# Forming a spectral unit's matrices on ScalarE and GpSimd during the first stage of a two-layer kernel, instead of on VectorE between the layers

## The chip, the cores and the metric

The kernel runs on one core of a Trainium2 chip. The metric is the device time of one execution in microseconds (us); the median of seven executions is compared. Engines are called by the profile's short names: PE (TensorE), ACT (ScalarE), DVE (VectorE), POOL (GpSimd), and SP, the engine whose queue issues the DMAs.

## The reference, cut to what matters

Two layers work on a tensor of 4 images, 128 channels and 64x64 pixels. Layer 0 is a convolutional front with a learned order of patches and a selective scan; layer 1 is a second scan with 256 states and then a spectral unit. The spectral unit has four branches (the first 1/1, 1/2, 1/4 and 1/8 of the sequence), each with matrices of its own, and the branches are added with four weights:

```python
s = sigma ** 0.25
out = einsum('btkd,k,kde->bte', U_plus, s, M_plus[i]) + einsum('btkd,k,kde->bte', U_minus, s, M_minus[i])
y_soft = softmax(log_weights + gumbel)
weights = one_hot(argmax(y_soft), 4) - y_soft + y_soft
out = sum over branches i of weights[i] * padded(out_i)
```

A token in the first eighth of the sequence belongs to all four branches, one in the last half to one only. So what the kernel needs for each filter k is, for each of four segments of the sequence, the weighted sum of the matrices of the branches that reach it, once for plus and once for minus, times sigma[k] to the power 0.25. It stores their sum and their difference. These matrices depend on the weights alone, not on x.

## The kernel before, in words

`conv_attn_hybrid` runs four parts in a row.

- `layer0_front` loops over the 4 images. For each it loads x (`xs`, L108), takes statistics on DVE (L111 to L125) and one power on POOL (`rs`, L127), writes the normalised image `xg` (DVE, L129), transposes it on PE and takes more statistics from PSUM (L149 to L157), takes another power on POOL (`r1`, L161), and then does two convolutions on PE (L96), each of eight tiles of 128x512. ACT empties each tile of PSUM through Gelu (L176 for the first convolution, L196 for the second). PSUM has four buffers for these tiles, so the matmuls of tile i need the buffer that ACT emptied of tile i-4. The second convolution needs the mean over all eight Gelu tiles (L181). Scores, an order and a gather by matmul (L206 to L258) end the image. The order of instructions on each engine is set here by a scheduler, which fills from the program in the order of its readiness; once built it is fixed, and each engine works through its own list in order.
- `layer0_scan` has an order written out by hand (`manual_schedule`). It ends with a store of `x2` (L430).
- `spectral_weights` forms the matrices. It loads three small vectors (L616 to L619) and, by some twenty DVE instructions of up to 128x4, gets the four branch weights `wt`; POOL takes the power of sigma (`sig`, L645). `branch_sums` (L647) forms running sums over the four branches with one multiplication and three multiply-adds on DVE. It is called once for the three matrices of `M_u` (to `mue`, stored as `mud`), and for each of 16 filters twice (plus and minus, tile `raw` to tile `sums`). Then DVE multiplies `sums` by `sig` (L668), adds and subtracts the two halves (L670, L671, tile `pq`), and SP stores both to DRAM as `pqd` (L673). `raw`, `sums` and `pq` have two buffers each.
- `layer1` again has an order written out by hand: eight weight and data loads, a projection, and then 8192 steps. Each step runs a scan of 128x1024 on DVE (L1097); POOL forms the scan's input for two steps at a time (L1085), and ACT its factors (L1094). The spectral unit's matmuls (L1045, L989) run beside the scan at a pace that the program sets, and read `pqd` (L956) and `mud` (L903) from DRAM.

Of the kernel before, what the change touches and what calls it, by code (L numbers as in the profile page):

```python
# [8 lines left out]
F32 = mybir.dt.float32  # L9
AF = mybir.ActivationFunctionType  # L10
ALU = mybir.AluOpType
# [6 lines left out]


@with_exitstack  # L20
def layer0_front(ctx: ExitStack, tc, ident, half, w, x, xnt, perm_t):

# [1 line left out]
    nc = tc.nc  # L26
    cp = ctx.enter_context(tc.tile_pool(name="a_c", bufs=1))
# [73 lines left out]
    def by_patch(t, oy):  # L101

        return t.rearrange("c (py px oy ox) -> c oy py px ox", px=16, oy=4, ox=4)[:, oy]

    for b in range(NB):

        xs = xp.tile([128, L], F32, tag="xs", name="xs")
        nc.sync.dma_start(xs, x[b])  # L108
        st = sm.tile([128, 8, 6], F32, tag="st", name="st")
        for q in range(8):  # L110
            nc.vector.bn_stats(st[:, q, :], xs[:, bass.ts(q, 512)])  # L111
# [61 lines left out]
        sums = sm.tile([128, 8], F32, tag="sums", name="sums")  # L173
# [426 lines left out]
NK = 16  # L600


@with_exitstack
def spectral_weights(ctx: ExitStack, tc, sigma, m_u, m_plus, m_minus, log_w, gumbel, pqd, mud):

    nc = tc.nc
    cp = ctx.enter_context(tc.tile_pool(name="w_c", bufs=1))  # L610
    mp = ctx.enter_context(tc.tile_pool(name="w_m", bufs=2))


    lw = cp.tile([128, 4], F32, name="lw")
    gb = cp.tile([128, 4], F32, name="gb")
    nc.sync.dma_start(lw, log_w.partition_broadcast(128))  # L616
    nc.sync.dma_start(gb, gumbel.partition_broadcast(128))
    sig = cp.tile([128, NK], F32, name="sig")
    nc.sync.dma_start(sig, sigma.partition_broadcast(128))  # L619
    nc.vector.tensor_tensor(lw, lw, gb, ALU.add)  # L620
    top = cp.tile([128, 1], F32, name="top")
    nc.vector.tensor_reduce(top, lw, AX, ALU.max)
    nc.vector.tensor_scalar(lw, lw, top, None, ALU.subtract)
    soft = cp.tile([128, 4], F32, name="soft")
    tot = cp.tile([128, 1], F32, name="tot")
    nc.scalar.activation(soft, lw, AF.Exp, accum_out=tot)
    nc.vector.reciprocal(tot, tot)
    nc.vector.tensor_scalar(soft, soft, tot, None, ALU.mult)
    nc.vector.tensor_reduce(top, soft, AX, ALU.max)
    hard = cp.tile([128, 4], F32, name="hard")  # L630
    nc.vector.tensor_scalar(hard, soft, top, None, ALU.is_equal)
    seen = cp.tile([128, 1], F32, name="seen")
    free = cp.tile([128, 1], F32, name="free")
    nc.vector.tensor_copy(seen, hard[:, 0:1])
    for i in range(1, 4):

        nc.vector.tensor_scalar(free, seen, -1.0, 1.0, ALU.mult, ALU.add)
        nc.vector.tensor_tensor(hard[:, i : i + 1], hard[:, i : i + 1], free, ALU.mult)
        nc.vector.tensor_tensor(seen, seen, hard[:, i : i + 1], ALU.max)
    wt = cp.tile([128, 4], F32, name="wt")  # L640
    nc.vector.tensor_tensor(wt, hard, soft, ALU.subtract)
    nc.vector.tensor_tensor(wt, wt, soft, ALU.add)
    quarter = cp.tile([128, NK], F32, name="quarter")
    nc.vector.memset(quarter, 0.25)
    nc.gpsimd.tensor_tensor(sig, sig, quarter, ALU.pow)  # L645

    def branch_sums(dst, src):  # L647

        nc.vector.tensor_scalar(dst[:, 3], src[:, 0], wt[:, 0:1], None, ALU.mult)
        for i in range(1, 4):  # L650
            nc.vector.scalar_tensor_tensor(
                dst[:, 3 - i], src[:, i], wt[:, i : i + 1], dst[:, 4 - i], ALU.mult, ALU.add
            )

    mu = mp.tile([128, 4, 3, 128], F32, name="mu", bufs=1)
    for i in range(4):
        nc.sync.dma_start(mu[:, i], m_u[i].rearrange("k d e -> d k e"))
    mue = mp.tile([128, 4, 3, 128], F32, name="mue", bufs=1)
    branch_sums(mue, mu)
    nc.sync.dma_start(mud, mue)  # L660
    for k in range(NK):
        raw = mp.tile([128, 2, 4, 128], F32, tag="raw", name="raw")
        nc.sync.dma_start(raw[:, 0], m_plus[:, k].rearrange("i d e -> d i e"))
        nc.sync.dma_start(raw[:, 1], m_minus[:, k].rearrange("i d e -> d i e"))
        sums = mp.tile([128, 2, 4, 128], F32, tag="sums", name="sums")
        for side in range(2):
            branch_sums(sums[:, side], raw[:, side])
        nc.vector.tensor_scalar(sums, sums, sig[:, k : k + 1], None, ALU.mult)  # L668
        pq = mp.tile([128, 2, 4, 128], F32, tag="pq", name="pq")
        nc.vector.tensor_tensor(pq[:, 0], sums[:, 0], sums[:, 1], ALU.add)  # L670
        nc.vector.tensor_tensor(pq[:, 1], sums[:, 0], sums[:, 1], ALU.subtract)  # L671
        for side in range(2):
            nc.sync.dma_start(pqd[k, side], pq[:, side])  # L673


@with_exitstack
# [564 lines left out]
@with_exitstack  # L1241
def conv_attn_hybrid(ctx: ExitStack, tc, w, out):
    nc = tc.nc
    const = ctx.enter_context(tc.tile_pool(name="const", bufs=1))
    dram = ctx.enter_context(tc.tile_pool(name="dram", bufs=1, space=DRAM))
    ident = const.tile([128, 128], F32, name="ident")
    make_identity(nc, ident)
    half = const.tile([128, 32], F32, name="half")
    nc.vector.memset(half, -0.5)
    x2 = dram.tile([NB, 128, L], F32, name="x2")  # L1250
    x3 = dram.tile([NB, 128, L], F32, name="x3")
    x = w["x"]
    with tc.tile_pool(name="ordered", bufs=1) as pool:
        xnt = dram.tile([NB, 128, 3 + L], F32, name="xnt")
        perm_t = pool.tile([128, NB, 2, 256], F32, name="perm_t")
        layer0_front(tc, ident, half, w, x, xnt, perm_t)
        layer0_scan(tc, ident, w, x, xnt, perm_t, x2)
    pqd = dram.tile([NK, 2, 128, 4, 128], F32, name="pqd")
    mud = dram.tile([128, 4, 3, 128], F32, name="mud")
    spectral_weights(  # L1260
        tc, w["sigma"], w["M_u"], w["M_phi_plus"], w["M_phi_minus"], w["log_weights"], w["gumbel"], pqd, mud
    )
    layer1(
        tc, ident, half, w["W_in"], w["W_delta"], w["W_B"], w["W_C"], w["W_out"], w["A"], w["phi"], pqd, mud,
        x2, x3, out,
    )
# [48 lines left out]
```

## Time and profile before

| what | value |
|---|---|
| median of 7 runs | 22131.32 us (22126.83 to 22139.19) |
| the profiled execution's own time | 22126.83 us |
| its span in the profile | 22125.0 us |
| busy: PE, DVE, ACT, POOL | 80%, 92%, 71%, 91% |
| `layer0_front` in the profile | 0 to about 776 us |
| `layer0_scan` | about 776 to 3002 us |
| `spectral_weights` | about 3001 to 3083 us |
| `layer1` | about 3083 us to the end |

The profiled execution is the fastest of the seven, 4.49 us under the median; its span is 1.8 us shorter than its time. A line such as "L471 POOL TENSOR_TENSOR v<-dx,bcb 128x1024 f32<-128x1024 f32 x512 | 1207.9, 2359 | ..." gives the line of the program, the engine, the operation, output and input with shape, the number of instructions, their busy time in us, the mean of one in ns, and after the second bar how long the engine sat idle before them and for whom. In the timeline, a line gives the start in us, the length in us, the engine and the instruction, and in brackets the idle time ahead of it and what ended it.

### The profile page before, as it was taken

The page shows a single profiled execution, that of the slowest core. Times are in us where ns is not written, and L with a number is a line of the kernel's source. Part 1 is how long each engine was busy: PE and PEld are TensorE (multiplying, and loading weights), DVE is VectorE, ACT ScalarE, POOL GpSimd, SP SyncE. Part 2 cuts the span into 40 slices and gives each one's busy share as a digit, 9 for nine tenths or more (in the row PEclk, how much of TensorE's full clock was granted, in tenths as well). Part 3 has the DMA queues.
Part 4 walks back from the last instruction along what each step waited for, and adds up shares of the span by engine and source line. Part 5 has one row for each costly group of instructions (what it writes and reads, how often), then busy time and mean ns, then how long its engine had stood idle before and what let it go on. Part 6 is the DMA issues. An engine that isn't in the chain of part 4 may idle for free.

```text
span 22125.0 us, 292872 instructions
## 1 busy us (share of the span) xinstructions
PE 17753.2 (80%) x99156; PEld 7770.0 (35%) x99156; DVE 20448.6 (92%) x11842; ACT 15727.5 (71%) x28971; POOL 20186.5 (91%) x5932
## 2 busy tenths in 40 slices
PE   8788844474867888886858888869598899999999
PEld 4444421131323333342323333324233334434344
DVE  3588879999999999999999999999999999999993
ACT  0477747777777777777777777777777777777773
POOL 0477759999999999999999999999999999999993
PEclk9899976586988999997979999979699999999999
DMA  0255544464656777675657777757577677777775
GB/s 27 78 139 140 140 136 151 151 197 151 206 186 200 218 222 218 218 220 180 213 173 217 220 219 218 220 179 229 164 226 222 218 233 233 232 230 230 229 226 153
DMA packets 2399971, 4238.15 MB, mean 192 GB/s; under 512 B 778200, under 2 KB 1235968, under 8 KB 2395136
## 3 DMA queue, kind: packets, MB, share of 16 engines
q1 hardware_dynamic: 2398464, 4219.40, 62.3%
q8 instruction: 781, 12.80, 0.2%
q14 instruction: 726, 5.95, 0.1%
HBM read 3600.52 MB, written 617.88 MB: 191 GB/s over the span
## 4 chain that ended last, share of the span: by engine, by line
DVE 50%; POOL 17%; PE 13%; ACT 10%; issue 7%; DMA 3%; SPq 0%; DVEq 0%; POOLq 0%; ACTq 0%
DVE s L1097 43%; POOL v L1085 16%; ACT da L1094 6%; PE conv L1045 5%; DVE states L493 3%; PE conv L96 2%; DMA yd<-ye 2%; PE yp L1114 2%; DVE p L497 2%; PE fin L989 1%; ACT f L485 1%; PE y L509 1%; PE mm L402 0%; ACT ye L1120 0%; ACT t L764 0%
## 5 line engine op out<-in xcount | busy, mean ns | idle before, releaser
L1085 POOL TENSOR_TENSOR v<-u,dlb 128x2044 f32<-128x2044 f32 x4096 | 18346.0, 4526 | 105.1 <-DMA dlb<-delta 81.0
L1097 DVE TENSOR_TENSOR_SCAN s<-da,v 128x1024 f32<-128x1024 f32 x8192 | 18055.4, 2268 | 380.3 <-ACT da L1094 308.2
L1094 ACT ACTIVATE da<-dlb,at 128x511 f32<-128x511 f32 x16384 | 11299.5, 690 | 2062.5 <-DVE s L1097 1597.2
L1045 PE MATMUL conv<-strip,tok 128*128 128x512 f32 (+3 forms) x20480 | 8640.2, 551 | 4.0 <-DMA strip<-in_phi 3.9
L1114 PE MATMUL yp<-s,c 128*32 128x256 f32 x65536 | 5015.8, 437 | 2971.5 <-DVE s L1097 1623.8
L1045 PEld LDWEIGHTS conv<-strip,tok 128*128 128x128 f32 x20480 | 3685.1, 192 | 4131.9 <-issue 3749.5
L1114 PEld LDWEIGHTS yp<-s,c 128*32 128x32 f32 x65536 | 1983.8, 121 | 6760.0 <-issue 1838.0
L1089 ACT COPY v<-vf 128x4 f32<-128x4 f32 x4096 | 813.5, 199 | 2259.3 <-DVE s L1097 2134.2
L471 POOL TENSOR_TENSOR v<-dx,bcb 128x1024 f32<-128x1024 f32 x512 | 1207.9, 2359 | 429.5 <-DVE states L493 425.5
L989 PE MATMUL fin<-conved,pq 128*128 128x512 f32 (+1 forms) x3200 | 1422.3, 540 | 11.9 <-ACT conved L1056 3.3
L493 DVE TENSOR_TENSOR_SCAN states<-f,v 128x1024 f32<-128x1024 f32 x512 | 1176.1, 2297 | 173.1 <-ACT f L485 124.0
L1120 ACT COPY ye<-yp 128x512 f32<-128x512 f32 x2048 | 1186.5, 579 | 142.9 <-DMA yd<-ye 125.0
L485 ACT ACTIVATE f<-dt,an 128x255 f32<-128x255 f32 x2048 | 973.4, 476 | 420.3 <-DVE states L493 369.6
L509 PE MATMUL y<-p,ident 128*128 128x512 f32 x2048 | 1003.9, 619 | 149.8 <-DVE p L497 144.6
L1056 ACT COPY conved<-conv 128x512 f32<-128x512 f32 x1344 | 778.5, 579 | 341.8 <-PE conv L1045 340.4
L497 DVE TENSOR_TENSOR p<-states,bcb 128x1024 f32<-128x1024 f32 x512 | 627.0, 1225 | 41.1 <-DVE states L493 2.2
L989 PEld LDWEIGHTS fin<-conved,pq 128*128 128x128 f32 x3200 | 532.1, 194 | 225.3 <-issue 163.5
L509 PEld LDWEIGHTS y<-p,ident 128*128 128x128 f32 x2048 | 367.3, 194 | 679.9 <-issue 358.3
L127 POOL TENSOR_TENSOR rs<-sq,half 128x1 f32<-128x1 f32 x4 | 2.2, 561 | 486.2 <-DVE sq L125 486.2
L402 PE MATMUL mm<-ow,yg 128*32 128x128 f32 x2048 | 282.0, 297 | 106.9 <-ACT om L406 105.4
L402 PEld LDWEIGHTS mm<-ow,yg 128*32 128x32 f32 x2048 | 236.0, 138 | 212.9 <-ACT om L406 128.4
L1005 DVE TENSOR_TENSOR xo<-xo,fin 128x512 f32<-128x512 f32 x32 | 21.3, 666 | 300.8 <-PE fin L997 300.8
(232 smaller groups left out, 6265.2 us busy)
## 6 DMA issues: line engine op xcount, KB each, us to landing
dlb<-delta SPq DMA_DIRECT2D x4096, 512.0 KB, 4.1
strip<-in_phi SPq DMA_DIRECT2D x1536, 448.0 KB, 4.8
yd<-ye SPq DMA_DIRECT2D x2048, 256.0 KB, 4.0
bcb<-bcd SPq DMA_DIRECT2D x1024, 256.0 KB, 4.2
strip<-in_phi SPq DMA_DIRECT2D x1024, 256.0 KB, 4.3
pq<-pqd SPq DMA_DIRECT2D x1088, 64.0 KB, 3.8
yt<-yd SPq DMA_DIRECT2D x4096, 4.0 KB, 3.3
pq<-pqd SPq DMA_DIRECT2D x256, 128.0 KB, 4.0
```

The source lines that it names most:

```text
L471: nc.gpsimd.tensor_tensor(v, ready[n][2][:, :, bass.ts(i, SUB)].unsqueeze(1).broadcast_to((128, 2, 2, SUB)), bc[:, 0].unsqueeze(2).broadca ...
L485: nc.scalar.activation(factors[j % 2][:, a, k, 1:], ready[n][1][:, k, SUB * i + 1 : SUB * i + SUB], AF.Exp, scale=an[:, k, 2 * g + a : 2 * ...
L493: nc.vector.tensor_tensor_scan(states.rearrange(flat), factors[j % 2].rearrange(flat), v.rearrange(flat), 0.0, ALU.mult, ALU.add)
L497: nc.vector.tensor_tensor(p, states, bc[:, 1].unsqueeze(2).broadcast_to((128, 2, 2, SUB)), ALU.mult)
L509: nc.tensor.matmul(t.rearrange("p k t -> p (k t)"), ident, p[:, a].rearrange("p k t -> p (k t)"), start=g == 0 and a == 0, stop=False, ski ...
L989: nc.tensor.matmul(fin[:, bass.ds(c0, w)], pq[:, n, :], u[:, bass.ds(c0, w)], start=begin and n == 0, stop=end and not partly, skip_group_ ...
L1045: nc.tensor.matmul(ps[:, skip:], tok[:, 1 - r if side else r, j, :], strip[:, bass.ds(c0 - lo, TS - skip)], start=src == sources[0] and j ...
L1085: nc.gpsimd.tensor_tensor(v[:, :, :, 1:], ready[0][:, :, 1:].unsqueeze(1).broadcast_to((128, VD, 2, TS - 1)), dl[:, :, 1:].unsqueeze(2).br ...
L1094: nc.scalar.activation(da[:, h, 1:], dl[:, d % VD, 1:], AF.Exp, scale=at[:, h, d : d + 1])
L1097: nc.vector.tensor_tensor_scan(s[:, d % GD].rearrange("p h t -> p (h t)"), da.rearrange("p h t -> p (h t)"), v[:, d % VD].rearrange("p h t ...
L1114: nc.tensor.matmul(yp[i // 2][bass.ts(q, 32), i % 2], c[:, h, t], s[:, :, h, t], start=h == 0, stop=h == 1)
L1120: nc.scalar.copy(ye, yp[j].rearrange("p i d t -> p i t d"))
```

## The change

The matrices are formed inside `layer0_front`. `spectral_weights` becomes a generator that yields after the `M_u` matrices and after each filter; the loop over images asks it for five pieces in each image, right after the load of that image. Its pools now live as long as the front's. The multiplications go from DVE to ACT (`Copy` with a scale, two sides at once, 128x256), with the branch weight and the power of sigma multiplied beforehand into a small tile `both`, so that the multiplication by `sig` alone falls away; the additions go to POOL, in place in `sums`, and so do the final sum and difference. The DRAM tensors are unchanged but are made earlier. The small computation of `wt` is unchanged and stays on DVE, now in the front.

```diff
-def layer0_front(ctx: ExitStack, tc, ident, half, w, x, xnt, perm_t):
+def layer0_front(ctx: ExitStack, tc, ident, half, w, x, xnt, perm_t, pqd, mud):
...
+    matrices = spectral_weights(
+        ctx, tc, w["sigma"], w["M_u"], w["M_phi_plus"], w["M_phi_minus"], w["log_weights"], w["gumbel"], pqd, mud
+    )
     for b in range(NB):
         xs = xp.tile([128, L], F32, tag="xs", name="xs")
         nc.sync.dma_start(xs, x[b])
+        for _ in range(5):
+            next(matrices, None)
...
-@with_exitstack
-def spectral_weights(ctx: ExitStack, tc, sigma, m_u, m_plus, m_minus, log_w, gumbel, pqd, mud):
+def spectral_weights(ctx, tc, sigma, m_u, m_plus, m_minus, log_w, gumbel, pqd, mud):
...
-    def branch_sums(dst, src):
-
-        nc.vector.tensor_scalar(dst[:, 3], src[:, 0], wt[:, 0:1], None, ALU.mult)
+    both = cp.tile([128, 4, NK], F32, name="both")
+    for i in range(4):
+        nc.vector.tensor_scalar(both[:, i, :], sig, wt[:, i : i + 1], None, ALU.mult)
+
+    def branch_sums(dst, src, weight):
+
+        for i in range(4):
+            nc.scalar.activation(dst(3 - i), src(i), AF.Copy, scale=weight(i))
         for i in range(1, 4):
-            nc.vector.scalar_tensor_tensor(
-                dst[:, 3 - i], src[:, i], wt[:, i : i + 1], dst[:, 4 - i], ALU.mult, ALU.add
-            )
+            nc.gpsimd.tensor_tensor(dst(3 - i), dst(3 - i), dst(4 - i), ALU.add)
...
-    branch_sums(mue, mu)
+    branch_sums(lambda r: mue[:, r], lambda i: mu[:, i], lambda i: wt[:, i : i + 1])
     nc.sync.dma_start(mud, mue)
+    yield
     for k in range(NK):
...
-        for side in range(2):
-            branch_sums(sums[:, side], raw[:, side])
-        nc.vector.tensor_scalar(sums, sums, sig[:, k : k + 1], None, ALU.mult)
+        branch_sums(lambda r: sums[:, :, r], lambda i: raw[:, :, i], lambda i: both[:, i, k : k + 1])
         pq = mp.tile([128, 2, 4, 128], F32, tag="pq", name="pq")
-        nc.vector.tensor_tensor(pq[:, 0], sums[:, 0], sums[:, 1], ALU.add)
-        nc.vector.tensor_tensor(pq[:, 1], sums[:, 0], sums[:, 1], ALU.subtract)
+        nc.gpsimd.tensor_tensor(pq[:, 0], sums[:, 0], sums[:, 1], ALU.add)
+        nc.gpsimd.tensor_tensor(pq[:, 1], sums[:, 0], sums[:, 1], ALU.subtract)
         for side in range(2):
             nc.sync.dma_start(pqd[k, side], pq[:, side])
+        yield
...
+        pqd = dram.tile([NK, 2, 128, 4, 128], F32, name="pqd")
+        mud = dram.tile([128, 4, 3, 128], F32, name="mud")
         perm_t = pool.tile([128, NB, 2, 256], F32, name="perm_t")
-        layer0_front(tc, ident, half, w, x, xnt, perm_t)
+        layer0_front(tc, ident, half, w, x, xnt, perm_t, pqd, mud)
         layer0_scan(tc, ident, w, x, xnt, perm_t, x2)
-    pqd = dram.tile([NK, 2, 128, 4, 128], F32, name="pqd")
-    mud = dram.tile([128, 4, 3, 128], F32, name="mud")
-    spectral_weights(
-        tc, w["sigma"], w["M_u"], w["M_phi_plus"], w["M_phi_minus"], w["log_weights"], w["gumbel"], pqd, mud
-    )
```

In the built program, the scheduler does not spread the sixteen filters over the four images as the loop asks for them. All sixteen stand inside the first image on every engine:

- ACT: the four copies for `mue`, 24 copies (filters 0 to 5), the table load and the first Gelu tile of convolution 1; then, between the Gelu tiles, 8 copies (filters 6, 7), tile 1, 8 (8, 9), tile 2, 12 (10 to 12), tile 3, 9 (13, 14 and a quarter of 15), tile 4, 3, and tiles 5 to 7.
- POOL: the power of sigma, `rs` of image 0, the three additions for `mue`, filters 0 to 5 (three additions and the two for `pq` each), `r1` of image 0, filters 6 to 15, and only then `rs` of image 1.
- SP: the load of image 0, the small vectors, `mu`, `raw` of filters 0 and 1, the load of image 1, then stores and loads mixed: the stores of filters 0 and 1 ahead of the loads of filters 2, 3 and 4; the stores of 2 and 3 ahead of the load of 5; those of 4 ahead of 6 and 7; of 5 ahead of 8; of 6 and 7 ahead of 9; and so on to the last stores, all ahead of the first image's own store `xnt`.
- DVE: about twenty small instructions between the statistics of image 0 and its transposes' statistics.
- At the other end, the first weight load of `layer1` stands just ahead of the store of `x2`, and the other loads just after it.

## The prediction

> **What bounds the kernel now.** I read the chain of waits first: it says which engine each stage hangs on. DVE and POOL carry most of it in `layer1`, but the change touches only two short stages, so I asked for busy times by stretch: image 0's first convolution, the gap after it, and the stretch between the layers.
>
> ```profile
> DVE 50%; POOL 17%; PE 13%; ACT 10%; issue 7%; DMA 3%; SPq 0%; DVEq 0%; POOLq 0%; ACTq 0%
> ```
> ```profile
> core 0: us, PE busy (x) PEld busy (x) DVE busy (x) ACT busy (x) POOL busy (x), PEclk, DMA share, GB/s
> 44.00:109.30 65.30, 65.23 (x144) 28.06 (x144) 22.23 (x102) 6.99 (x17) 5.45 (x1) 0.96 0.00 0
> 109.30:112.40 3.10, 0.60 (x4) 0.43 (x4) 1.69 (x8) 3.05 (x5) 0.00 (x0) 1.00 0.00 0
> ...
> 3001.60:3083.30 81.70, 0.00 (x0) 0.00 (x0) 68.74 (x200) 0.30 (x2) 2.91 (x1) 0.52 0.73 238
> ```
>
> Between the layers PE does nothing for 81.7 us, ACT and POOL next to nothing: DVE alone works, 68.7 us of it. In the convolution PE is full, and ACT and POOL have 58 and 60 us to spare. The waits of the stretch between the layers and its timeline tell what holds `layer1` back:
>
> ```profile
> DVE sums L649 <- DMA raw<-in_M_phi_plus: 6.1, 13, 0.6
> ...
> DVE ones L717 <- DMA pqd<-pq: 2.3, 1, 2.3
> ```
> ```profile
> 3001.79 0.37 SPq L430 DMA_DIRECT2D x<-xs  x1
> ```
> ```profile
> 3080.28 0.68 DVE L671 TENSOR_TENSOR pq<-sums 128x512 f32<-128x512 f32 x1
> 3083.28 0.17 DVE L717 MEMSET ones<- 128x128 f32 x1 [2.32 <-DMA pqd<-pq]
> ...
> 3083.42 0.33 SPq L707 DMA_DIRECT2D win<-in_W_in  x1
> ...
> 3086.32 0.47 SPq L783 DMA_DIRECT2D t<-x  x1
> ```
>
> `layer1` starts when the last `pqd` store lands, and its first piece of work is the load of `t` at 3086.32. Everything before it is in series.
>
> **What the skill says.** (1) GPSIMD Engine Reference, Elementwise: side-by-side cycle accounting: an f32 add of 2048 per partition takes 4497 ns. The trace agrees, 4526 ns for 128x2044 (L1085). (2) PSUM, Engine vs sequencer instructions: the queues of ScalarE, VectorE and GpSimd are strictly first in, first out. So a Gelu tile behind matrix copies waits for whatever those wait for. The trace shows no instruction of these engines overtaking. (3) GPSIMD Engine Reference, Specifications: GpSimd shares its SBUF interfaces with VectorE. No run here shows a slowdown from it: L378 takes 2348 ns and L471, beside DVE's scan, 2359. (4) TensorE, What's actually happening: after some microseconds of idleness PE runs at half its clock until it has been busy again. The trace agrees: after the thin stretch of 20.7 us ahead of image 1's convolution, its first weight loads are 0.85 us apart, then 0.43; after the 3.1 us ahead of convolution 2 there is none of it.
>
> **The change, part by part.**
>
> *What is removed.* `layer1`'s seven first loads need no `pqd` now. In the built order they follow the `x2` store of 3001.79, one of them ahead of it. Five at 0.51 us (the spacing at 3083.8 to 3086.3) lie between store and `t`: 3001.8 + 0.4 + 5 x 0.51 = 3004.7, so 81.6 us sooner. The 1 MB store in front of them on the DMA engines takes at most 2.3 us at the 440 GB/s of the start's loads; I take half: **80.5 us gained** (79.3 to 81.6). If `layer1`'s memory were released only with that store's landing (3.84 us in the chain), 78 are left.
>
> *Small DVE work in the front.* The twenty instructions for `wt` and `both` cost 0.15 to 0.23 us each. Of those ahead of `xg`, six fall into DVE's waits for PE and POOL (0.7 us each); seven do not: 1.4 us. Five more among the copies to `xp`, 1.0, and four for `both`, 0.8. Image 0's convolution starts 3.2 us late. POOL's power of sigma (2.9 us) runs while DVE still takes statistics, before `rs` is due. `wt` is ready at 31.2 + 1.4 + 1.0, about 34; `both` at 36.
>
> *The price of one filter.* POOL, from these rows:
>
> ```profile
> L471 POOL TENSOR_TENSOR v<-dx,bcb 128x1024 f32<-128x1024 f32 x512 | 1207.9, 2359 | 429.5 <-DVE states L493 425.5 <-DMA bcb<-bcd 3.5
> ...
> L161 POOL TENSOR_TENSOR r<-ve,half 128x32 f32<-128x32 f32 x4 | 21.8, 5444 | 108.7 <-DVE ve L160 108.7
> ```
>
> 2359 ns for 1024 and 4526 for 2044 give 2.12 ns an element and 0.18 us fixed; dependent additions in the timeline stand 0.08 us further apart. So an addition of 256 takes 0.80 us, one of 512 1.27: 3 x 0.80 + 2 x 1.27 = 4.94 us. ACT: 4 copies at 0.48 (128x255 in L485 takes 476 ns) = 1.9 us. SP: 0.92 for two loads, 0.94 for two stores, `raw` landing 3.1 us after its issue, all as before. POOL is the slow stage: ACT may be two filters ahead (two `sums` buffers), no more.
>
> *Walking the built order.* `mue`: two copies of 0.56, three additions of 1.07: POOL is through at 38.5. Filters 0 and 1 end at 48.4. The loads for filter 2 stand behind their stores on SP: issued by 49.6, landed 52.7, copied, so POOL idles 5.3 us; filters 2 to 5 end at 74.0 (with 0.4 us more of idling). `r1`, 5.45 us, ends at 79.4; its followers on DVE (8.3 us of normalising, 3.7 of statistics) are done by 92, 20 us before they are needed. Filters 6 to 13 take 40.4 us (0.1 each of idling from the same SP order): 119.8.
>
> ACT's Gelu tiles wait in that line. In the profile before, they are:
>
> ```profile
> 54.77 0.69 ACT L176 ACTIVATE f<-conv,b 128x512 f32<-128x512 f32 x1 [0.52 <-PE conv L96]
> ...
> 109.28 0.70 ACT L176 ACTIVATE f<-conv,b 128x512 f32<-128x512 f32 x1 [7.01 <-PE conv L96]
> ```
>
> Tile 0 is now emptied at 73 (behind filter 5), tile 1 at 78, tile 2 at 96, tile 3 at 107. PE needs their buffers for tiles 4 to 7 at 81, 89, 97 and 104.5: PE stalls once, by some 3 us, ahead of tile 7. The end is set by ACT: filter 15's first copy needs the `sums` of filter 13 (119.8) and follows filter 14's copies, 121.2; tile 4 at 121.9, three copies, tiles 5 to 7: the last Gelu ends at **125.7 instead of 110.0, 15.7 us late**. The 3.2 us of the late start are inside this. Convolution 2 needs the mean over all eight tiles, so this is on the path. PE idles some 12 us there instead of 3.1; half clock then costs what it costs convolution 1 (65.2 us against 8 x 7.79 = 62.3): **2.9**. Sum: 18.6.
>
> *What is free.* POOL ends filter 15 at 130, 80 us before `rs` of image 1 (213.6); SP's last store is out by then too, 80 us before `xnt`. Images 1 to 3, `layer0_scan` and `layer1`'s loop keep their instructions and order: nothing.
>
> *Sum.* 80.5 - 18.6 = **61.9 us less** than the profiled execution: 22126.8 becomes 22064.9. That execution is 4.5 us under the median, so the median becomes 22069.4.
>
> *Unseen prices, from both sides.* No row shows POOL additions of 256 with two strides, or beside DVE's two-port copies and statistics. Below: at 0.8 of my prices the last Gelu ends at 114.2, and under 0.75 it ends at 113 whatever they are, as the late convolution sets it. Above: at 1.1, 131.5; at 1.25, 141.7. A gain below zero in DVE's or SP's waits is excluded: nothing there gets less. `layer1`'s DRAM addresses shift; its loop is 19,040 us long, and the runs shown spread by 6 us either side, which I allow it.
>
> **The rivals.**
>
> *A. As walked: 22069* (POOL prices at 0.85 to 1.25 of mine give 22061 to 22085). For it: the idle stretch is in series, POOL's prices come from the same operation. Chance 0.68.
>
> *B. Fully hidden.* POOL is quick enough (0.8 or less), the Gelu tiles come back in time, only the 3.2 us of small DVE work remain: 22131.3 - 80.5 + 3.2 = 22054. For it: 60 us of idle POOL in that stretch. Against it: filters 0 to 15 cost 79 us there plus 5.4 for `r1`, and the window is 66. Chance 0.20.
>
> *C. The gain is mostly given back, no change.* Either POOL at 1.3 to 1.9 of my price (44 us or less are then left), or `layer1`'s start waiting for something else, such as its weights behind the store and the scan's last memory: 22088 to 22131. Against it: the idle stretch ended with the `pqd` landing to 0.2 us. Chance 0.08.
>
> *D. Slower: the Gelu queue.* ACT's line of tiles behind matrix copies becomes the bound of image 0. The gain is gone when the last Gelu ends at 188 (110 + 80.5 - 2.9), which takes POOL at 1.9 of my price, 9.4 us a filter; at 2.5 times it ends near 232 and the time is 22131.3 - 80.5 + 122 + 2.9 = 22176. For it: two-input additions on a port shared with DVE. Against it: DVE is busy only a third of that stretch, and 2359 ns beside its scan shows none of it. Chance 0.04.
>
> *That the change doesn't do what it says* is half true already: nothing is spread over the images. That the matrices leave the stretch between the layers is plain from the order.
>
> **How the numbers follow.** The likeliest is A: 22069. The range takes A's bounds and B less the runs' spread: 22050 to 22090. A measurement of this kernel can tell about 0.2%, 44 us, from no change. Faster by more: A, B and a little of C, 0.90; within: the rest of C, 0.06; slower: D, 0.04.
>
> **What would show it.** Right: `layer1`'s load of `t` follows the end of `layer0_scan` by some 3 us; POOL additions of 256 near 0.72 us and of 512 near 1.27; the last Gelu of image 0 near 126 us; convolution 2 of image 0 with a slow start; images 1 to 3 as long as before (187.8 us). Wrong: an idle gap between the layers over 10 us; Gelu tiles in time (B) or past 145 us (C, D); a longer loop in `layer1`.

## The result, and the profile after

The changed kernel takes **22074.49 us** (median of 13 runs, 22067.22 to 22079.0); beside it the kernel before took 22134.42 us (33 runs, 22125.21 to 22140.54). The ratio is 0.9973, with a 95% interval of 0.9966 to 0.9980: 59.9 us less. The forecast was 22069 us, the range 22050 to 22090. The profiled execution of the changed kernel took 22080.38 us, its span is 22078.7 us, and the granted clock is 0.903 as before. In the changed kernel a line of the first stage stands 6 lines lower than before, one of `layer1` 9 lower.

The chain of waits has hardly moved: the change concerns about 200 us of 22,000.

```profile
DVE 50%; POOL 17%; PE 14%; ACT 9%; issue 6%; DMA 3%; SPq 0%; DVEq 0%; POOLq 0%; ACTq 0%
```

The same stretches as before show it. These are the busy times of core 0 in image 0's first convolution, in the gap ahead of convolution 2, and between the layers:

```profile
core 0: us, PE busy (x) PEld busy (x) DVE busy (x) ACT busy (x) POOL busy (x), PEclk, DMA share, GB/s
46.76:125.06 78.30, 64.89 (x144) 27.56 (x144) 43.93 (x106) 31.81 (x75) 67.52 (x69) 0.96 0.57 185
125.06:128.36 3.30, 0.85 (x4) 0.68 (x4) 1.87 (x4) 2.81 (x4) 3.14 (x4) 0.50 0.17 64
3023.70:3033.39 9.69, 0.00 (x0) 0.00 (x0) 0.22 (x5) 0.00 (x0) 0.29 (x1) 0.66 0.87 285
```

The stretch between the layers has shrunk from 81.7 us to 9.7, in which hardly anything but DMAs runs. The first convolution has grown from 65.3 to 78.3 us with the same 144 matmuls and 64.9 us of PE in it: PE is no longer full there. POOL nearly is, with 67.5 of 78.3 us. DVE's busy time has doubled from 22.2 to 43.9 us, though no multiplication or addition of the matrices was given to it there; this comes back below.

The start of `layer1` in the timeline (start in us, length, engine; SPq is SP's DMA queue):

```profile
3023.01 0.33 SPq L716 DMA_DIRECT2D win<-in_W_in  x1
...
3023.76 0.33 SPq L436 DMA_DIRECT2D x<-xs  x1
3024.15 0.41 SPq L720 DMA_DIRECT2D wbd<-in_W_B  x1
...
3028.32 0.41 SPq L792 DMA_DIRECT2D t<-x  x1
...
3033.42 1.09 PE L796 MATMUL mm<-ident,t 128*128 128x128 f32 x4 [10.58 <-DMA t<-x]
```

One weight load stands ahead of the scan's last store, five between it and the load of `t`, as in the built order. From the store to PE's first transpose it is now 3033.42 - 3023.76 = 9.66 us; before it was 3091.67 - 3001.79 = 89.88. The gain there is **80.2 us**. The store itself comes 22.0 us later than before (3023.76 against 3001.79), of which the front accounts for 18.0: the scan's first load, `win`, is issued at 794.23 us instead of 776.21. The other 4.0 us lie between `win` and the store, where nothing was changed; that stretch took 2225.6 us before, 2229.5 after, and 2224.8 (nopq) to 2235.6 (frontdve) in the experiments.

The front's 18 us come from the Gelu tiles, ACT's lines of `f` in image 0:

```profile
72.47 0.69 ACT L182 ACTIVATE f<-conv,b 128x512 f32<-128x512 f32 x1
76.34 0.68 ACT L182 ACTIVATE f<-conv,b 128x512 f32<-128x512 f32 x1
95.09 0.67 ACT L182 ACTIVATE f<-conv,b 128x512 f32<-128x512 f32 x1
105.94 0.68 ACT L182 ACTIVATE f<-conv,b 128x512 f32<-128x512 f32 x1
121.19 0.67 ACT L182 ACTIVATE f<-conv,b 128x512 f32<-128x512 f32 x1
...
124.37 0.69 ACT L182 ACTIVATE f<-conv,b 128x512 f32<-128x512 f32 x1
138.41 0.69 ACT L202 ACTIVATE f<-conv,b 128x512 f32<-128x512 f32 x1 [10.24 <-PE conv L97]
```

Before, these eight stood 7.8 us apart and ended at 110.0. Now they come when ACT's matrix copies let them. The last ends at 125.1, and the first tile of convolution 2 comes at 138.41 instead of 120.54. The waits of the first 140 us say for whom ACT waits (total in us, times, longest), and what of it reaches PE:

```profile
ACT sums L660 <- DMA raw<-in_M_phi_minus: 32.7, 6, 13.5
ACT sums L660 <- POOL pq L679: 20.8, 5, 8.0
...
DVE mean L187 <- ACT f L182: 9.8, 1, 9.8
...
PE conv L97 <- ACT f L182: 3.2, 2, 2.8
```

PE is stalled for 3.2 us only, because the accumulators in PSUM hold the tiles; what costs is that the last tiles are emptied late, and that the mean waits for them.

More of ACT's waiting is put down to loads of `raw` (32.7 us) than to POOL (20.8). But on SP these loads stand behind the stores of filters that POOL has only just finished:

```profile
82.88 6.41 SPq L681 DMA_DIRECT2D pqd<-pq  x4
89.79 0.39 SPq L673 DMA_DIRECT2D raw<-in_M_phi_plus  x1
```

The last of these four stores has the sum and difference of filter 7, which POOL ends at 88.9. POOL itself waits little: after the 5.7 us ahead of filter 2 only 1.9 us more, in three waits.

### The profile page after: what moved, and what is told of

The parts are those of the page before. It is cut to its first block, busy times and chain, and to the rows that moved or that the text cites. A ratio compares the mean times of both kernels' runs of the same rounds, so it can differ in the third digit from the quotient of the medians.

```text
span 22078.7 us, 292873 instructions
## 1 busy us (share of the span) xinstructions
PE 17777.6 (81%) x99156; PEld 7778.5 (35%) x99156; DVE 20403.2 (92%) x11666; ACT 15758.4 (71%) x29040; POOL 20264.0 (92%) x6015
## 4 chain that ended last, share of the span: by engine, by line
DVE 50%; POOL 17%; PE 14%; ACT 9%; issue 6%; DMA 3%; SPq 0%; DVEq 0%; POOLq 0%; ACTq 0%
DVE s L1106 44%; POOL v L1094 16%; ACT da L1103 6%; PE conv L1054 5%; DVE states L499 3%; PE conv L97 2%; DMA yd<-ye 2%; PE yp L1123 2%; DVE p L503 1%; PE fin L998 1%; ACT f L491 1%; PE y L515 1%; PE mm L408 1%; ACT t L773 0%; ACT ye L1129 0%
```

## The experiments

The theory has two parts. **The place brings the gain**: 80 us of matrix work in series become work beside a convolution. **POOL's pace gives some back**: ACT's copies may be two filters ahead of POOL, and the Gelu tiles stand behind those copies. The rivals are that faster engines bring the gain, that SP's loads and stores cost the front its 18 us, or that VectorE could have done as well there. Eight kernels were run, in two groups of four, with the kernel before at 22134.07 and 22133.87 us beside them. In the traces I compare two times: the end of the last Gelu tile of image 0's first convolution (its start is given) and the issue of `win`, at which the front is over.

### Without the arithmetic: none

```diff
-        sums = mp.tile([128, 2, 4, 128], F32, tag="sums", name="sums")
-        branch_sums(...)
-        pq = mp.tile([128, 2, 4, 128], F32, tag="pq", name="pq")
-        nc.gpsimd.tensor_tensor(pq[:, 0], sums[:, 0], sums[:, 1], ALU.add)
-        nc.gpsimd.tensor_tensor(pq[:, 1], sums[:, 0], sums[:, 1], ALU.subtract)
...
-            nc.sync.dma_start(pqd[k, side], pq[:, side])
+            nc.sync.dma_start(pqd[k, side], raw[:, side])
```

> The arithmetic of the sixteen filters is left out: each raw tile is stored as it came, and the loads, stores, mue and the small vectors stay in the front. Theory: only the small DVE work is left of the front's loss, so the last Gelu of image 0 ends near 113 us and the time is 22134 - 80 + 3 = 22057 us: the ceiling of what moving the matrices can bring. Rival (loads and stores of 8 MB beside the front cost time by themselves): the last Gelu stays well past 113 us and the time above 22065 us.

Measured: 22058.85 us (22047.96 to 22062.93), ratio 0.9966 (0.9952 to 0.9979). The last Gelu tile starts at 111.43, `win` at 778.76, only 2.6 us later than before. All loads and stores of the 16 filters are still there, so their traffic alone does not cost the front its 18 us. (The stores no longer wait for POOL, so the waits in SP's queue are not tested by this.) This is the ceiling of the change, some 16 us better than the changed kernel.

### POOL's work halved: nopq

```diff
-        pq = mp.tile([128, 2, 4, 128], F32, tag="pq", name="pq")
-        nc.gpsimd.tensor_tensor(pq[:, 0], sums[:, 0], sums[:, 1], ALU.add)
-        nc.gpsimd.tensor_tensor(pq[:, 1], sums[:, 0], sums[:, 1], ALU.subtract)
+        pq = sums
```

> The last sum and difference are left out, sums is stored as it is: POOL has three additions of 256 a filter, 2.4 us instead of 4.9, with ACT's copies and all loads and stores as before. Theory (POOL's pace sets when the Gelu tiles are emptied): the chain is through before convolution 1 is, the last Gelu of image 0 ends near 113 us, 22058 us. Rival (ACT's copies or the order on SP set it): the last Gelu stays at 120 us or later, above 22068 us.

Measured: 22051.32 us (22050.44 to 22055.4), ratio 0.9963 (0.9951 to 0.9976). In ACT's timeline the tiles still bunch, but they are through:

```profile
100.27 0.67 ACT L182 ACTIVATE f<-conv,b 128x512 f32<-128x512 f32 x1
...
109.76 0.67 ACT L182 ACTIVATE f<-conv,b 128x512 f32<-128x512 f32 x1
...
111.48 0.68 ACT L182 ACTIVATE f<-conv,b 128x512 f32<-128x512 f32 x1
```

The last starts at 111.48, as in none, and `win` at 778.53. ACT's copies are all kept here, so ACT's own work is not the bound. POOL's time per filter, halved, is enough to take away all of the delay but that of the late start. The stores and the loads behind them come sooner in this run too, so it tests POOL together with what follows POOL on SP.

### Loads further ahead: raw4

```diff
-        raw = mp.tile([128, 2, 4, 128], F32, tag="raw", name="raw")
+        raw = mp.tile([128, 2, 4, 128], F32, tag="raw", name="raw", bufs=4)
```

> Four raw buffers instead of two, so that loads need not stand behind the stores of the filters before. Theory, by walking the built order with the durations of the changed kernel's trace (4.87 us a filter on POOL): POOL's idling of 5.7 us ahead of filter 2 goes, but ACT's order becomes 32 copies, tile 0, 12, tile 1, 8, tile 2, 12, tiles 3 to 7; tile 3 is emptied at 113.8, PE waits for its buffer ahead of tile 7 and ends it at 121.7, and the last Gelu ends at 122.4 instead of 125.1; convolution 2 then starts after a short gap and without the half clock: 5 us less than the changed kernel, 22069 us. Rival (loads set the pace): with all loads early the last Gelu ends at 113 and the time is 22058 us.

Measured: 22071.94 us (22059.7 to 22083.84), ratio 0.9971 (0.9960 to 0.9981), not to be told from the changed kernel. The tiles did not do what was expected:

```profile
75.38 0.69 ACT L182 ACTIVATE f<-conv,b 128x512 f32<-128x512 f32 x1
...
116.77 0.67 ACT L182 ACTIVATE f<-conv,b 128x512 f32<-128x512 f32 x1
...
127.36 0.69 ACT L182 ACTIVATE f<-conv,b 128x512 f32<-128x512 f32 x1 [7.84 <-PE conv L97]
```

I expected the last at 122.4, and it came at 127.36. With more buffers the built order puts more copies ahead of each tile; POOL was done sooner, at 124.85, but PE waited for ACT 11.1 us in three waits instead of 3.2 in two. Nor did the waits for data go away: ACT waits for `raw` 30.4 us, after 32.7, and POOL still idles 4.4 us ahead of one filter, since the later loads stand behind stores on SP as before. So this run shows that more buffers do not help in this order; it does not show what earlier data would bring.

### The filters spread over the images: spread

```diff
+            mine = mp.tile([128, 4, NK], F32, tag="mine", name="mine")
+            nc.vector.scalar_tensor_tensor(
+                mine..., pin[0].broadcast_to((128, 4 * NK)), 0.0, both..., ALU.mult, ALU.add,
+            )
...
-        for _ in range(5):
-            next(matrices, None)
...
+        pin[0] = gm
+        for _ in range(5):
+            next(matrices, None)
```

The weights are passed through a product of zero with the image's mean `gm`, so that a filter cannot start ahead of its image. The images get four, five, five and two filters.

> Each image's filters are tied to that image by a scale tile made from its own mean (a multiplication by zero and an addition on DVE, 64 elements), so that the scheduler can't pull all sixteen into image 0: filters 0 to 3 stay there, 4 to 8, 9 to 13 and 14, 15 go to images 1 to 3. Theory (Gelu tiles wait in ACT's queue behind sixteen filters in one image): with four or five filters an image POOL is through some 30 us after the image's statistics, the Gelu tiles come in time in every image, the last Gelu of image 0 ends near 113 us and convolution 2 starts without the half clock; left are the 3.2 us of small DVE work and 0.2 us an image: 22134 - 80 + 4 = 22058 us, 16 us under the changed kernel. Rival (the 18 us lost in the front are the price of the work itself, by ports shared with DVE or by DMA traffic): they are lost in other places, the time stays at 22074 us.

Measured: 22058.51 us (22054.42 to 22069.82), ratio 0.9967 (0.9954 to 0.9979). The last Gelu tile of image 0 starts at 110.78. But `win` is issued at 788.22, where 780 was expected (4 us late): each of the images 1 to 3 is some 3.3 us longer than before. The groups of image 1's patches show why; this is 215.5 to 224 us of spread:

```profile
L664 POOL TENSOR_TENSOR sums<-sums 128x256 f32<-128x256 f32 x4 | 5.6, 1401 | 0.2
L139 DVE COPY xp<-xg 128x1024 f32<-128x1024 f32 x4 | 5.6, 1454 | 0.0
...
L134 DVE TENSOR_SCALAR xg<-xs,gm,rs 128x4096 f32<-128x4096 f32 x1 | 2.8, 2806 | 0.7 <-POOL rs L132 0.7
```

The copies into patches take 1454 ns each; in image 0, without POOL beside them, they take 688. POOL's additions of 256 take 1401 ns on average instead of 727. Both engines slow each other down, and PE waits for the patches.

### The filters past the copies: spread2

```diff
-        pin[0] = gm
+        pin[0] = xp1[:, 12:13]
```

An element that the last copy writes now releases the filters.

> As spread, four filters in each image, but the images' filters wait for the copies of xg into patches instead of for gm. In spread those copies took 1454 ns each in images 1 to 3 beside GpSimd's additions (688 ns without), and the additions of 256 took 1530 ns (727 without); the write of xg took 2806 ns instead of 2415: 3.45 us an image. If the two engines slow each other down there, and nowhere else in the image, moving GpSimd's work past the copies brings both back to 690 and 727 ns, the first load of the scan comes at 778 us instead of 788, and the time is about 22048 us, 10 us under spread. Rival (the 3.4 us an image come from ScalarE's order or from SP's): the copies are 690 ns again but the scan still starts at 786 to 788 us, and the time stays at 22058 us.

Measured: 22053.02 us (22052.37 to 22064.17), ratio 0.9964 (0.9952 to 0.9977). The same groups over the same stretch:

```profile
L139 DVE COPY xp<-xg 128x1024 f32<-128x1024 f32 x4 | 2.5, 690 | 0.0
L134 DVE TENSOR_SCALAR xg<-xs,gm,rs 128x4096 f32<-128x4096 f32 x1 | 2.4, 2415 | 0.7 <-POOL rs L132 0.7
L664 POOL TENSOR_TENSOR sums<-sums 128x256 f32<-128x256 f32 x2 | 1.5, 726 | 6.9 <-ACT sums L662 6.9
```

All three durations are back, and `win` is issued at 777.79 (778 was expected), 10.4 us sooner than in spread. That settles that the copies were slowed by what ran beside them: only the moment of the filters' work was moved. It was moved on ACT and on POOL together, but ACT's copies took their 492 ns in spread too, while POOL's additions were slowed with DVE's copies. The medians of the two differ by 5.5 us, less than the spread of their runs, so the 10.4 us are shown by the trace and not by the times. Spread2 leaves nothing out and is 21 us under the changed kernel: it reaches the ceiling that none and nopq show, and is the best version found.

### The engines alone: between

The generator is run to its end between the layers, where VectorE's version stood:

```diff
+    with ExitStack() as mctx:
+        for _ in spectral_weights(mctx, tc, w["sigma"], ..., pqd, mud):
+            pass
```

> Only the engines change, not the place: the matrices are formed by ScalarE and GpSimd as in the changed kernel, but where VectorE formed them before, between the two layers. If the place brings the gain, nothing hides GpSimd's line here: 3.2 us for mue, 16 filters at 4.87 us and some 9 us of idling behind SP's order give about 90 us where VectorE's stretch took about 70, so 22134 + 20 = 22154 us, slower than before by about 0.1%. The rival, that the gain comes from faster engines or from VectorE being freed, would make it faster than before, 22074 to 22120 us.

Measured: 22149.47 us (22144.6 to 22158.66), ratio 1.0007 (0.9999 to 1.0016): 15.6 us more than the 22133.87 beside it, 5 less than expected. The stretch between the layers, and its largest groups:

```profile
3001.40:3103.50 102.10, 0.00 (x0) 0.00 (x0) 5.74 (x28) 29.70 (x70) 80.10 (x85) 0.52 0.62 195
```
```profile
L657 POOL TENSOR_TENSOR sums<-sums 128x256 f32<-128x256 f32 x48 | 34.7, 723 | 9.1 <-ACT sums L655 6.3
...
L674 POOL TENSOR_TENSOR pq<-sums 128x512 f32<-128x512 f32 x16 | 20.2, 1261 | 0.0
L673 POOL TENSOR_TENSOR pq<-sums 128x512 f32<-128x512 f32 x16 | 20.2, 1261 | 1.2
```

POOL is busy for 80.1 us where DVE was busy for 68.7, and `t` is loaded at 3103.57 instead of 3086.32. The two engines are slower than the one that they replace. The engines alone bring nothing; the interval just touches no change.

### The place alone: frontdve

```diff
-        for i in range(4):
-            nc.scalar.activation(dst(3 - i), src(i), AF.Copy, scale=weight(i))
+        nc.vector.tensor_scalar(dst(3), src(0), weight(0), None, ALU.mult)
         for i in range(1, 4):
-            nc.gpsimd.tensor_tensor(dst(3 - i), dst(3 - i), dst(4 - i), ALU.add)
+            nc.vector.scalar_tensor_tensor(dst(3 - i), src(i), weight(i), dst(4 - i), ALU.mult, ALU.add)
...
-        nc.gpsimd.tensor_tensor(pq[:, 0], ...)
-        nc.gpsimd.tensor_tensor(pq[:, 1], ...)
+        nc.vector.tensor_tensor(pq[:, 0], ...)
+        nc.vector.tensor_tensor(pq[:, 1], ...)
```

> Only the place changes, not the engine: VectorE forms all matrices inside the first stage, with its former operations. In the built order mue and four filters stand on VectorE ahead of the patches of image 0, so convolution 1 should start about 17 us late (2.3 + 4 x 2.8 us and waits for raw, 3.2 us of small work); the other twelve filters lie beside the convolution, where VectorE was busy 22 of 65 us. Theory (the place brings the gain, and what counts in the front is what stands ahead of PE): 22134 - 80 + 18 = 22072 us, like the changed kernel, with all eight Gelu tiles emptied 7.8 us apart. Rival (VectorE becomes the bound of the front): over 22085 us and Gelu tiles in time but convolution 2 late. Second rival (VectorE's slack hides all): 22055 us.

Measured: 22075.19 us (22071.26 to 22080.93), ratio 0.9973 (0.9962 to 0.9984), the same as the changed kernel. Its loss has another shape:

```profile
70.50 0.69 ACT L182 ACTIVATE f<-conv,b 128x512 f32<-128x512 f32 x1
...
124.47 0.70 ACT L182 ACTIVATE f<-conv,b 128x512 f32<-128x512 f32 x1 [7.01 <-PE conv L97]
141.08 0.69 ACT L202 ACTIVATE f<-conv,b 128x512 f32<-128x512 f32 x1 [9.86 <-PE conv L97]
```

All tiles are emptied in time, each after a wait for PE. But the first comes 15.7 us late (70.50 against 54.77), because `mue` and four filters stand on DVE among the statistics of the patches, and PE starts the convolution at 60.25 instead of 44.01. After the last tile the mean is held up: filter 15 stands ahead of it on DVE.

```profile
125.10 1.53 DVE L661 SCALAR_TENSOR_TENSOR sums<-raw,both,sums 128x256 f32<-128x256 f32 x3
...
127.27 0.68 DVE L678 TENSOR_TENSOR pq<-sums 128x512 f32<-128x512 f32 x1
...
128.19 0.17 DVE L187 TENSOR_REDUCE mean<-sums 128x1 f32<-128x8 f32 x1
```

That is about 3 us more than before, and the half-clock start of convolution 2 follows, so `win` is 21.0 us late (797.18). The place is worth its 80 us whichever engine works there.

### Sum and difference on VectorE: dvepq

```diff
-        nc.gpsimd.tensor_tensor(pq[:, 0], ...)
-        nc.gpsimd.tensor_tensor(pq[:, 1], ...)
+        nc.vector.tensor_tensor(pq[:, 0], ...)
+        nc.vector.tensor_tensor(pq[:, 1], ...)
```

> The sum and the difference of each filter go from GpSimd to VectorE, all else as in the changed kernel, and nothing is left out. GpSimd's line falls from 4.87 to about 2.35 us a filter. If GpSimd's pace sets the lateness of the Gelu tiles, the last Gelu of image 0 ends near 112 us and the time is about 22053 us (22048 to 22060), 20 us under the changed kernel. The rival: VectorE, first in first out, now waits for GpSimd's additions ahead of statistics and normalising, and gives part back: 22062 us or more, with waits of VectorE for sums of over 5 us in image 0.

Measured: 22072.15 us (five runs of 22067.09 to 22078.64 and one of 22215.04, which widens the interval), ratio 0.9982 (0.9963 to 1.0001). I expected 22053, and the rival came true: the last Gelu tile starts at 124.06. The delay arises ahead of convolution 1, in DVE's and PE's timelines:

```profile
40.76 1.19 DVE L678 TENSOR_TENSOR pq<-sums 128x512 f32<-128x512 f32 x1 [2.81 <-POOL sums L662]
...
52.85 1.20 DVE L678 TENSOR_TENSOR pq<-sums 128x512 f32<-128x512 f32 x1 [1.20 <-POOL sums L662]
```
```profile
59.64 64.38 PE L97 MATMUL conv<-xg,d 128*128 128x512 f32 x144 [8.76 <-DVE stx L159]
```

The sums and differences of the first four filters stand on DVE among the statistics of image 0's patches. DVE waits there for POOL's additions, PE waits for the statistics, and the convolution starts at 59.64 instead of 44.01. From there on its 144 matmuls run without a wait for ACT: the 15.6 us of the late start are the whole delay of the last tile (14.8 us). The tiles do queue behind ACT's copies here too, one of them behind a stand of ACT of 7.9 us (tile 2 at 89.27), but that costs PE nothing. In all DVE waits for POOL's additions 20.1 us, in eleven waits. So the run does not show what less work on POOL would bring by itself; that was nopq. Taking half of POOL's line away helps only if the new place does not bring a queue of its own.

## Why the prediction was right, and where it was off

**The gain between the layers**, forecast at 80.5 us, was 80.2. Its parts were not all right: from the store to the load of `t` the forecast had 2.9 us and the trace has 4.56, since two of SP's issues took 0.91 and 1.48 us; the 1.1 us set aside for the store ahead of them covered most of that.

**POOL's price**, the number that all else hung on, was forecast from two rows of other stages at 4.94 us a filter. The groups over the first 140 us:

```profile
L662 POOL TENSOR_TENSOR sums<-sums 128x256 f32<-128x256 f32 x48 | 34.9, 727 | 10.1 <-ACT sums L660 7.6
L679 POOL TENSOR_TENSOR pq<-sums 128x512 f32<-128x512 f32 x16 | 20.8, 1299 | 0.0
L678 POOL TENSOR_TENSOR pq<-sums 128x512 f32<-128x512 f32 x16 | 20.3, 1267 | 1.3
```

Additions of 256 take 727 ns and those of 512 take 1267 (forecast 0.72 and 1.27); the 1299 of one group come from its last addition, which took 1.77 us. In the timeline one filter takes 4.87 us.

**The walk** held throughout: `mue` ends at 37.8 (38.5), POOL idles 5.68 us ahead of filter 2 (5.3), `r1` ends at 79.2 (79.4), filter 13 at 119.2 (119.8), and the last Gelu tile at 125.1 (125.7). PE stalled once by 2.8 us ahead of tile 7 (3). The start of convolution 1 is 2.75 us late (3.2), and the half-clock start of convolution 2 costs 2.8 us (2.9): from the last tile to the second of convolution 2 it is 21.82 us, before 19.04. In sum the front lost 18.0 us, forecast 18.6.

**The sum** was forecast at 61.9 us; the medians differ by 59.9. The two profiled executions differ by only 46.3, though `t` is loaded 58.0 us sooner: from that load to the end the loop of `layer1` took 19038.7 us before and 19050.4 after. The experiments, with the same `layer1`, took 19033.3 (none) to 19041.6 (frontdve), which points to this execution and not to the change; it is also 5.9 us above the median of its kernel.

**What was wrong: the work on DVE beside POOL.** The forecast named what POOL's additions might cost beside DVE as an unseen price, but put the other side, what DVE's work would cost beside POOL, at nothing. I read the Trainium skill's GPSIMD Engine Reference, section Specifications, for the shared SBUF interfaces and set the point aside because POOL showed no slowdown beside the scan. The page names the condition: contention "with DVE instructions in a 2-port perf mode or with two SBUF inputs". The scan was a poor stand-in: the kernel keeps one of its two inputs, the factors, in PSUM, so it has one input in SBUF only. And only POOL's durations were looked at, not DVE's. The forecast had the normalising of `x1` at 8.3 us, done by about 88, and DVE's statistics done by 92. The group of 75 to 125 us shows otherwise:

```profile
L172 DVE TENSOR_SCALAR x<-x,mv,r 128x128 f32<-128x128 f32 x32 | 28.8, 975 | 21.7 <-POOL r L167 21.7
```

Each of the 32 takes 975 ns, and they end at 108. In the kernel before each takes 340 and in none, with POOL idle beside them, 348; in nopq, with POOL half as busy and all of ACT's copies kept, 500. POOL's additions kept their 727 ns there. The page's second condition fits dvepq, where DVE's additions of two tensors from SBUF went from 0.69 to 1.2 us. The normalising and the patch copies of spread read one tensor from SBUF, so that condition is not theirs; that they run in the mode that the first one names, no trace shows. The statistics ended at 112.0 rather than 92, so the 20 us of cover that I had counted were used up. It cost nothing, because the mean they could have held up was itself late, at 125.2. That this error did not show in the time was luck.

**The rivals.** B (fully hidden, 22054) was not the case, but its number is what nopq (22051) and spread2 (22053) measured once the tiles no longer stood behind POOL. C and D asked for POOL at 1.3 times my price or more, and it was at 0.99.

## What to carry to other kernels

Where one stretch leaves all engines but one idle, the gain is in the place: moving the work beside another stage brought 80 us, while the choice of engines brought nothing (22075 with VectorE, 22074 with ScalarE and GpSimd). Price then the slowest engine of the moved work, per piece, and walk the queue of whatever shares an engine with it: here eight evacuations behind the copies decided how much was given back, and spreading the pieces over the images took it back. (VectorE with the pieces spread in the same way was not run, so for the best version the choice of engines stays open.) Before hiding work on GpSimd, look at what VectorE does at that moment, price both engines, and put it beside operations that are not slowed by it.

## What was not expected of the hardware

- DVE and POOL slowed each other down in some pairs and not in others. Copies of 128x1024 f32 on DVE went from 688 to 1454 ns and POOL's additions from 727 to 1401 (spread). The 128x128 normalising went from 340 to 975 while POOL kept its 727 (the changed kernel). DVE's additions of 128x512 went from 0.69 to about 1.2 us in places beside POOL (dvepq). DVE's statistics of 128x512 took 674 ns beside POOL's additions and 679 in the kernel before.
- The same gap of about 3.1 us of little PE work ahead of convolution 2 was followed by a half-clock start in some kernels and not in others. In none, nopq, spread, spread2 and dvepq it cost 1.7 us in all four images (20.73 us from the last tile to the second of convolution 2, against 19.05), and in none it was given back at the next first convolution (73.56 against 75.36 us). The period of an image stayed at 187.7 us (187.8 before). What decides it stays open.
